# Transform along H with one load of y for both parts, two column halves in two PSUM banks, and the inverse along H beside the first MLP product

## The chip, the cores and the metric

The kernel runs on one core of a Trainium2 chip. The metric is the device time of one execution in microseconds (us). TensorE (PE) multiplies out of SBUF into PSUM, which has eight banks; VectorE (DVE) and ScalarE (ACT) empty PSUM; GpSimd (POOL) works on SBUF; SyncE (SP) issues nearly all DMAs. Everything is float32, and the profile shows every float32 matmul as two records, and as many weight loads (PEld).

## The reference

Two layers work on an image x of 2 x 768 x 64 x 64 (batch, channel, height H, width W). Layer 0 is a convolution block with a state space scan; the change does not touch it. Layer 1 is a spectral MLP:

```python
xf = rfft2(groupnorm(x), norm='ortho')            # 64 x 33 frequencies, complex
xr, xi = xf.real, xf.imag                         # 32 blocks of 24 channels
x1r = relu(xr @ w1[0] - xi @ w1[1] + b1[0])       # 24 -> 96 in each block
x1i = relu(xi @ w1[1] + xr @ w1[0] + b1[1])
x2r = softshrink(x1r @ w2[0] - x1i @ w2[1] + b2[0])
x2i = softshrink(x1i @ w2[1] + x1r @ w2[0] + b2[1])
x = x + irfft2(complex(x2r, x2i), norm='ortho')
```

Each Fourier transform is a product with a constant 64-point matrix: along W, then along H, and back in the other order.

## The kernel before, in words

`layer0` fills some three quarters of the time. `layer1` begins at about 3405 us. All its instructions are written in the order in which each engine runs them (`tc.manual_schedule()`), so an engine works strictly down its list, and waits where an operand or a buffer is not ready.

**Ahead of the loop** (3405 to 3515 us) the list `forward_w(0)` takes image 0 through the transform along W: 16 slabs of four rows, each loaded by SP (L585), normalized on DVE in six instructions (L624, tile fx), transposed on PE (pt, L635), copied to SBUF (xc), multiplied by the matrix fw (py, L642), copied to yw and stored to DRAM (yspec, L645). pt and py use PSUM tiles of the tag "aux" with three buffers. `evict` (L610, L612) copies them out, in turn on DVE and on ACT.

**The loop** has 192 steps. A *group* is six columns of W frequencies (`KWS`) of one image; the last group of an image has three, and the first one of an image begins with the frequencies 0 and 32, whose spectrum along W is real (`g.real`), so their columns of y hold 64 rows and not 128. A group has 16 steps (hp), each with two of the 32 channel blocks. Step n does, in this order:

1. `hidden` of step n: the first MLP product, ph (L798), four matmuls from zf, in 64-row halves of the array, into three banks; then bias and relu into hid, on ACT (L807, two) and DVE (L805, one).
2. `spectrum` of step n+1: the transform along H. For each column j, y's 64 channels are the stationary operand, and the real and imaginary halves of the matrix fh are the moving one, 64 elements each. The two matmuls of a column write the two partition halves of one PSUM tile, mz (tag "pz", one bank, L769). Four copies bring it into zf: two on DVE (L783), two on ACT (L785), written in the order DVE, ACT, ACT, DVE.
3. `out` of step n-1: the second MLP product, mo (L814), three matmuls for each of up to three pieces. Between the pieces stand the `bits`, a share of a background list: during the first 72 steps `forward_w(1)` (pt and py of image 1, as above), from step 112 on `inverse_w(0)` (ipo, L683, added to the image by DVE, L687, and stored). Steps 72 to 111 and the last have none.
4. `shrink` of step n-1: bias on DVE (L831), soft shrink on POOL (L836, L837) into z.

Once a group is done, `inverse_h` goes through the next group's even steps from hp 2 on: each call multiplies two columns of z, in the two row halves of the array, by the inverse matrix ih (pv, L729: four matmuls of 384 moving elements into two aux tiles), and `evict` copies them into vo, one on DVE and one on ACT; every second call stores vo on SP (L744, L746). The call stands in the middle of that step's bits, and thus between pieces of mo, or behind the last piece where there are no bits.

The last group's `inverse_h` and `inverse_w(1)` follow the loop as a tail (from about 4597 us).

PSUM before: aux 3 banks, mz 1, ph 3, mo 1, eight in all.

Of the kernel before, what the change touches and what calls it, by code (L numbers as in the profile page):

```python
# [9 lines left out]
F32 = mybir.dt.float32  # L10
# [5 lines left out]
B, DM, H, W = 2, 768, 64, 64  # L16
# [10 lines left out]
NHP, KG, DP = 16, 6, 32 * 32  # L27
# [4 lines left out]
def spectral_kernel(tc, a, out):  # L32
# [5 lines left out]
    with ExitStack() as top:  # L38
# [56 lines left out]
        with ExitStack() as ctx:  # L95
            layer1(ctx, tc, a, x1_d, y_d, v_d, outr, ident, gm1, gr1)
# [465 lines left out]
def layer1(ctx, tc, a, x1_d, y_d, v_d, outr, ident, gm1, gr1):  # L562

    nc = tc.nc
# [4 lines left out]
    ps = ctx.enter_context(tc.tile_pool(name="ps1", bufs=1, space=PSUM))  # L569
    fw = wp.tile([128, 128], F32, name="fw")  # L570
    fh = wp.tile([128, 128], F32, name="fh")
# [11 lines left out]
    def load_slab(b, q):  # L583
        slabs[b, q] = p2.tile([128, NCT, 256], F32, tag="slab", name=f"fx_{b}_{q}", bufs=5)
        nc.sync.dma_start(slabs[b, q], x1_d[b][:, :, q * 256 : (q + 1) * 256])  # L585
# [26 lines left out]
            nc.scalar.copy(out, psum)  # L612

    def aux(shape, name):
        return ps.tile(shape, F32, tag="aux", name=name, bufs=3)


    def forward_w(b):
# [9 lines left out]
        def turn_over(k, g):  # L628
            if g == 0:
                cols[k] = p2.tile([128, DM], F32, tag="xc", name=f"xc_{b}_{k}")  # L630
            xt = slabs[b, k // 2]
            pt = aux([128, 3, 128], f"pt_{b}_{k}_{g}")
            for j in range(3):
                at = (k % 2) * 128
                nc.tensor.transpose(pt[:, j, :], xt[:, 3 * g + j, at : at + 128], ident)  # L635
            evict(cols[k][:, g * 384 : (g + 1) * 384], pt.rearrange("p j c -> p (j c)"))

        def transform(k, g):
            rows[k] = yws[k % 3]
            py = aux([128, 384], f"py_{b}_{k}_{g}")  # L640
            half = slice(g * 384, (g + 1) * 384)
            nc.tensor.matmul(py, fw, cols[k][:, half], start=True, stop=True)  # L642
            evict(rows[k][:, 16 * g : 16 * g + 16, :GC], py.rearrange("p (n c) -> p n c", c=GC))
            if g == 1:
                nc.sync.dma_start(  # L645
                    y_d[b][2 * k : 2 * k + 2].rearrange("h k c -> (h k) c"),
                    rows[k].rearrange("p n c -> p (n c)"),
                )
# [19 lines left out]
    def inverse_w(b):  # L668
        last = L // 256
        vs, xs = {}, {}  # L670

        def load(q):
            vs[q] = p2.tile([128, 2, DM], F32, tag="slab", name=f"iv_{b}_{q}", bufs=5)
            xs[q] = p2.tile([128, NCT, 256], F32, tag="slab", name=f"ix_{b}_{q}", bufs=5)
            nc.sync.dma_start(  # L675
                vs[q], v_d[b][4 * q : 4 * q + 4].rearrange("(k h) w c -> (h w) k c", h=2)
            )
            nc.sync.dma_start(xs[q], x1_d[b][:, :, q * 256 : (q + 1) * 256])  # L678

        def transform(q, ct):  # L680
            po = aux([128, 2, 128], f"ipo_{b}_{q}_{ct}")
            for k in range(2):
                nc.tensor.matmul(  # L683
                    po[:, k, :], vs[q][:, k, ct * 128 : (ct + 1) * 128], iw, start=True, stop=True
                )
            xt = xs[q][:, ct, :]
            nc.vector.tensor_add(xt, xt, po.rearrange("p k t -> p (k t)"))  # L687
            if ct == NCT - 1:
                nc.sync.dma_start(outr[b, :, :, q * 256 : (q + 1) * 256], xs[q])  # L689

        todo = [lambda: load(0)]
        for q in range(last):
            if q + 1 < last:
                todo.append(lambda q=q: load(q + 1))
            for ct in range(NCT):
                todo.append(lambda q=q, ct=ct: transform(q, ct))
        return todo
# [58 lines left out]
    class Step:  # L756
# [4 lines left out]

        def spectrum(self):
            g, nk = self.g, len(self.g.kws)
            pz = ps.tile([128, KG, H], F32, tag="pz", name=f"mz_{self.n}")
            for j in range(nk):
                kn = H if g.real[j] else 128
                cols = g.y[:kn, j, self.hp * 64 : self.hp * 64 + 64]
                for ri in range(2):
                    nc.tensor.matmul(  # L769
                        pz[64 * ri : 64 * ri + 64, j, :],  # L770
                        cols,
                        fh[:kn, ri * H : (ri + 1) * H],
                        start=True,
                        stop=True,
                    )
            self.zf = p3.tile([128, KG * H], F32, tag="zf", name=f"zf_{self.n}")
            for ri in range(2):
                for e in range(2):
                    to = slice(64 * e + 32 * ri, 64 * e + 32 * ri + 32)
                    src = pz[64 * ri + 32 * e : 64 * ri + 32 * e + 32, :nk, :]  # L780
                    dst = self.zf[to, : self.nt]
                    if e == ri:
                        nc.vector.tensor_copy(dst, src.rearrange("p j h -> p (j h)"))  # L783
                    else:
                        nc.scalar.copy(dst, src.rearrange("p j h -> p (j h)"))  # L785

        def hidden(self):
            nt = self.nt
# [54 lines left out]
    def at(n):  # L843
        return steps[n] if 0 <= n < len(steps) else None

    with tc.manual_schedule():
        for do in forward_w(0):
            do()
        load_slab(1, 0)
        groups[0].load()  # L850
        later = {0: forward_w(1), per + NHP: inverse_w(0)}
        pace = {0: 5 * NHP - 8, per + NHP: 4 * NHP + 2}
        fill, todo, given, begun = [], [], 0, 0
        groups[1].load()
        steps[0].spectrum()
        for n in range(len(steps) + 2):
            now, before, after = at(n), at(n - 1), at(n + 1)
            gi, hp = divmod(n, NHP)
            if n in later:
                assert given == len(todo)  # L860
                todo, given, begun, span = later[n], 0, n, pace[n]
            due = min(len(todo), -(-len(todo) * (n + 1 - begun) // span))
            bits = todo[given:due]
            given = due
            if hp == 2 and gi > 0:
                fill = groups[gi - 1].inverse_h()
            if hp >= 2 and hp % 2 == 0 and fill:
                bits.insert(len(bits) // 2, fill.pop(0))
            if hp == 1 and 0 < gi and gi + 1 < len(groups):
                groups[gi + 1].load()  # L870
            if now is not None:
                if hp == 0:
                    now.g.open()
                now.hidden()
            if after is not None:
                after.spectrum()
            cuts = [len(bits) * i // 4 for i in range(5)]
            for j in range(4):
                for do in bits[cuts[j] : cuts[j + 1]]:
                    do()  # L880
                if before is not None and j < 3 and 128 * j < before.nt:
                    before.out(j)
            if before is not None:
                before.shrink()
        for do in groups[-1].inverse_h():
            do()
        assert given == len(todo)
        for do in inverse_w(1):
            do()
# [96 lines left out]
```

## Time and profile before

| | us |
|---|---|
| median of three runs | 4713.02 (4712.79 to 4720.27) |
| profiled execution | 4721.7, span 4719.9 |
| PE busy | 4416.7 (94%) |
| weight loads (PEld) busy | 3224.1 (68%) |
| DVE busy | 3714.8 (79%) |
| ACT busy | 2349.2 (50%) |
| POOL busy | 922.3 (20%) |
| mz, L769: records, mean | 3968 of form 128\*64 at 227 ns, 256 of form 64\*64 at 238 ns |
| zf copies of 32x384 | DVE 320 at 554 ns, ACT 320 at 470 ns |
| zf copies of 32x192 | DVE 64 at 355 ns, ACT 64 at 310 ns |
| pv, L729 | 528 records of 64 rows, mean 508 ns |

A form like 128\*64 names the rows and columns of the array that a matmul uses. Records of one group overlap: two matmuls in different parts of the array run at the same time, and a record's duration includes the time until its last result is out. The time that a run of matmuls takes is therefore read from the start of its first record to the start of the next run's first. The share of busy time is an average over stages with different limits, and the two layers have little in common.

### The profile page before, as it was taken

How to read it: one execution, taken by the hardware profiler on the slowest of the kernel's cores; microseconds unless marked ns; L12 is line 12 of the kernel's file. 1: busy time of each engine (PE TensorE's matmuls, PEld its weight loads, DVE VectorE, ACT ScalarE, POOL GpSimd, SP SyncE). 2: the span in 40 equal slices, each digit the busy share in tenths (PEclk: the TensorE clock that was granted, in tenths of full speed). 3: DMA queues.
4: the chain of work that ended last, by engine and by line, in shares of the span. 5: the costliest groups of instructions: out<-in, count | busy, mean ns of one | idle time of the engine just before them, and what ended most of it. 6: DMA issues, size and time to landing. Idle time of an engine off the chain costs nothing. (4 is left out here: it accounts for less than half of the span.)

```text
span 4719.9 us, 78500 instructions
## 1 busy us (share of the span) xinstructions
PE 4416.7 (94%) x28368; PEld 3224.1 (68%) x28368; DVE 3714.8 (79%) x5630; ACT 2349.2 (50%) x4811; POOL 922.3 (20%) x1681
## 2 busy tenths in 40 slices
PE   5989999999999999999999999996679999999995
PEld 4567666777777677777777777774547666777774
DVE  4499999899999999899999999998455555444443
ACT  0365555565656656566566665664024444433330
POOL 1022211122222211122222222221201112222220
PEclk9999999999999999999999999998789999999998
DMA  6567777566666666566666666662383442346429
GB/s 235 172 184 216 219 216 211 180 199 200 207 196 194 201 192 207 168 202 204 204 207 192 204 203 202 195 188 84 138 272 103 114 127 82 81 130 175 134 75 330
DMA packets 517665, 854.31 MB, mean 181 GB/s; under 512 B 60369, under 2 KB 402017, under 8 KB 510113
## 3 DMA queue, kind: packets, MB, share of 16 engines
q1 hardware_dynamic: 514208, 833.66, 58.8%
q0 software_dynamic: 3072, 15.63, 0.9%
q8 instruction: 229, 3.75, 0.3%
q14 instruction: 156, 1.27, 0.1%
HBM read 606.87 MB, written 114.03 MB: 153 GB/s over the span
## 5 line engine op out<-in xcount | busy, mean ns | idle before, releaser
L444 PE MATMUL po<-y,wo 128*128 128x256 f32 x4608 | 1084.2, 386 | 92.1 <-DVE o L455 92.1
L245 PE MATMUL pi<-x,wi 128*128 128x256 f32 (+2 forms) x4608 | 1090.0, 386 | 1.1 <-ACT x L226 1.1
L444 PEld LDWEIGHTS po<-y,wo 128*128 128x128 f32 x4608 | 886.3, 193 | 251.2 <-DVE o L455 113.9
L245 PEld LDWEIGHTS pi<-x,wi 128*128 128x128 f32 x4608 | 851.5, 191 | 217.6 <-issue 102.2
L373 DVE TENSOR_TENSOR_SCAN hs<-da,hs 128x1028 f32<-128x1028 f32 x384 | 883.3, 2300 | 46.6 <-DVE hs L369 0.5
L352 ACT ACTIVATE da<-dl,acol 128x256 f32<-128x256 f32 x1536 | 639.9, 497 | 2.6 <-DVE hs L373 1.1
L284 PE MATMUL pc<-pair,wc 128*64 128x256 f32 x4608 | 594.0, 390 | 21.1 <-DMA pair<-win 10.9
L383 POOL TENSOR_TENSOR hc<-hc 128x512 f32<-128x512 f32 x384 | 488.4, 1272 | 605.1 <-DVE hc L382 595.6
L377 POOL COPY state<-hs 128x4 f32<-128x4 f32 x360 | 104.6, 291 | 1985.2 <-DVE hs L373 1985.2
L783 DVE COPY zf<-mz 32x384 f32<-32x384 f32 (+1 forms) x384 | 200.0, 521 | 368.0 <-ACT zf L785 185.2
L284 PEld LDWEIGHTS pc<-pair,wc 128*64 128x64 f32 x4608 | 305.5, 137 | 268.9 <-issue 149.8
L382 DVE TENSOR_TENSOR hc<-hs,bc 128x1024 f32<-128x1024 f32 x384 | 468.0, 1219 | 0.0
L369 DVE TENSOR_TENSOR hs<-du,bc 128x1024 f32<-128x1024 f32 x384 | 465.7, 1213 | 0.7 <-DMA bc<-bc_d 0.7
L260 ACT COPY win<-pi 128x256 f32<-128x256 f32 (+2 forms) x384 | 137.9, 359 | 654.9 <-PE pi L245 613.8
L297 DVE SCALAR_TENSOR_TENSOR pc<-win,vec,pc 128x256 f32<-128x256 f32 x768 | 373.7, 487 | 83.9 <-PE pc L284 66.9
L814 PE MATMUL mo<-w,hid 128*128 128x96 f32 (+1 forms) x3264 | 435.8, 279 | 0.7 <-DVE v L831 0.7
L814 PEld LDWEIGHTS mo<-w,hid 128*128 128x128 f32 (+1 forms) x3264 | 391.2, 189 | 52.2 <-issue 25.6
L807 ACT ACTIVATE hid<-ph,b 128x384 f32<-128x384 f32 (+1 forms) x384 | 212.7, 555 | 307.6 <-PE ph L798 306.6
L798 PE MATMUL ph<-zf,w 64*128 64x384 f32 (+3 forms) x1536 | 316.4, 496 | 3.6 <-ACT zf L785 3.6
L345 ACT ACTIVATE dl<-pz,vec 128x256 f32<-128x256 f32 x384 | 170.5, 473 | 214.8 <-PE pz L341 212.1
L836 POOL TENSOR_SCALAR cl<-v 128x288 f32<-128x288 f32 (+1 forms) x224 | 85.0, 380 | 933.3 <-DVE v L831 920.9
L785 ACT COPY zf<-mz 32x384 f32<-32x384 f32 (+1 forms) x384 | 170.3, 443 | 170.9 <-DVE zf L783 168.6
(119 smaller groups left out, 4909.8 us busy)
## 6 DMA issues: line engine op xcount, KB each, us to landing
wi<-in_win_dram SPq DMA_DIRECT2D x384, 384.0 KB
wo<-wout_d SPq DMA_DIRECT2D x192, 768.0 KB
pair<-win SPq DMA_DIRECT2D x1536, 66.0 KB
wc<-in_wcv_dram SPq DMA_DIRECT2D x384, 192.0 KB
bc<-bc_d SPq DMA_DIRECT2D x32, 1024.0 KB
yspec<-yw SPq DMA_DIRECT2D x64, 512.0 KB
xo<-in_x_dram SPq DMA_DIRECT2D x192, 128.0 KB
x<-o SPq DMA_DIRECT2D x192, 128.0 KB
```

What stands on the lines that cost most here:

```text
L245: nc.tensor.matmul(self.pi[:, : self.tn], self.win[dt][:, ct, :], self.x[:, ct, : self.tn], start=(ct == 0), stop=(ct == NCT - 1),)
L284: nc.tensor.matmul(pc[64 * h : 64 * h + 64, :T], self.wcv[dt][:, h, dx, :], pair[:, h, :, dx : dx + W], start=(dx == 0), stop=(dx == 2),)
L297: nc.vector.scalar_tensor_tensor(acc if dx < 2 else u, wins[dt][:, 2 : 2 + ROWS, dx : dx + W], vec[:, dt, 6 + dx : 7 + dx], acc, ALU.mult, ...
L352: nc.scalar.activation(das[dt % 4][:, s, 1:], self.dl[dt], AF.Exp, scale=acol[:, dt, s : s + 1])
L369: nc.vector.tensor_mul(hs[:, :, 1:], self.du.unsqueeze(1).to_broadcast([128, NS, T]), self.bc[:, :NS, :])
L373: nc.vector.tensor_tensor_scan(flat, self.da[dt].rearrange("p s t -> p (s t)"), flat, 0.0, ALU.mult, ALU.add)
L382: nc.vector.tensor_mul(hc, hs, self.bc[:, NS:, :])
L383: nc.gpsimd.tensor_add(hc[:, 0:2, :], hc[:, 0:2, :], hc[:, 2:4, :])
L444: nc.tensor.matmul(self.po[ct][:, :T], self.out[ct][0][:, dt, :], self.y[dt], start=(dt == 0), stop=(dt == NDT - 1),)
L798: nc.tensor.matmul(to, w1[rows, self.hp, cols], self.zf[rows, :nt], start=True, stop=True)
L807: nc.scalar.activation(hid, ph[q][:, :nt], AF.Relu, bias=bias)
L814: nc.tensor.matmul(self.po[:n, j, :], self.hid[:, q, j * 128 : j * 128 + n], w2[:, self.hp, q, :], start=(q == 0), stop=(q == 2),)
```

## The change

`aux` gets two buffers, and mz two tiles (tags pz0 and pz1), so PSUM stays at eight banks.

`spectrum` does one matmul for each column, with the whole of fh (128 elements) as the moving operand, so both parts come from one load of y. The columns are split in two halves of hk (three of six, two and one of three). The first half writes partitions 0 to 63 of pz0, the second half partitions 64 to 127 of pz1, and they are issued in turns: j = 0, 3, 1, 4, 2, 5, or 0, 2, 1. A tile holds real and imaginary parts side by side, so each copy into zf takes 32 partitions with three runs of 64: four copies of pz0 on DVE, four of pz1 on ACT.

In the loop, a call of `inverse_h` is taken out of the bits, and stands between `hidden` and `spectrum`.

```diff
     def aux(shape, name):
-        return ps.tile(shape, F32, tag="aux", name=name, bufs=3)
+        return ps.tile(shape, F32, tag="aux", name=name, bufs=2)
...
-            pz = ps.tile([128, KG, H], F32, tag="pz", name=f"mz_{self.n}")
-            for j in range(nk):
-                kn = H if g.real[j] else 128
-                cols = g.y[:kn, j, self.hp * 64 : self.hp * 64 + 64]
-                for ri in range(2):
-                    nc.tensor.matmul(
-                        pz[64 * ri : 64 * ri + 64, j, :],
-                        cols,
-                        fh[:kn, ri * H : (ri + 1) * H],
-                        start=True,
-                        stop=True,
-                    )
+            pz = [
+                ps.tile([128, KG // 2, 2, H], F32, tag=f"pz{i}", name=f"mz_{self.n}_{i}")
+                for i in range(2)
+            ]
+            hk = (nk + 1) // 2
+            for j in sorted(range(nk), key=lambda j: j % hk):
+                kn, side = H if g.real[j] else 128, 64 * (j // hk)
+                nc.tensor.matmul(
+                    pz[j // hk][side : side + 64, j % hk].rearrange("p r h -> p (r h)"),
+                    g.y[:kn, j, self.hp * 64 : self.hp * 64 + 64],
+                    fh[:kn, :],
+                    start=True,
+                    stop=True,
+                )
             self.zf = p3.tile([128, KG * H], F32, tag="zf", name=f"zf_{self.n}")
-            for ri in range(2):
+            for side, ks in ((0, hk), (1, nk - hk)):
                 for e in range(2):
-                    to = slice(64 * e + 32 * ri, 64 * e + 32 * ri + 32)
-                    src = pz[64 * ri + 32 * e : 64 * ri + 32 * e + 32, :nk, :]
-                    dst = self.zf[to, : self.nt]
-                    if e == ri:
-                        nc.vector.tensor_copy(dst, src.rearrange("p j h -> p (j h)"))
-                    else:
-                        nc.scalar.copy(dst, src.rearrange("p j h -> p (j h)"))
+                    for ri in range(2):
+                        to = slice(64 * e + 32 * ri, 64 * e + 32 * ri + 32)
+                        rows = slice(64 * side + 32 * e, 64 * side + 32 * e + 32)
+                        src = pz[side][rows, :ks, ri, :]
+                        dst = self.zf[to, side * hk * H : (side * hk + ks) * H]
+                        dst = dst.rearrange("p (j h) -> p j h", h=H)
+                        if side == 0:
+                            nc.vector.tensor_copy(dst, src)
+                        else:
+                            nc.scalar.copy(dst, src)
...
-            if hp >= 2 and hp % 2 == 0 and fill:
-                bits.insert(len(bits) // 2, fill.pop(0))
...
                 now.hidden()
+            if hp >= 2 and hp % 2 == 0 and fill:
+                fill.pop(0)()
             if after is not None:
                 after.spectrum()
```

## The prediction

> **What bounds the kernel now.** I read the busy time by stage first, since the page's averages mix two layers. The changed code runs in the last quarter of the span (4719.9 us; the profiled execution took 4721.7 us, 8.7 us above the median of 4713.02, so I add differences to the median).
>
> ```profile
> 3405.00:3515.00 110.00, 90.20 (x320) 49.37 (x320) 69.36 (x160) 30.68 (x64) 6.05 (x2) 0.90 0.73 259
> 3552.00:4590.00 1038.00, 1036.68 (x10028) 736.18 (x10028) 517.75 (x1092) 433.55 (x876) 230.05 (x430) 1.00 0.41 114
> ```
>
> Columns: stretch, length, busy time of PE, weight loads, DVE, ACT, POOL, then granted clock, DMA share, GB/s. In the second row, the loop over 192 steps, PE works 1036.68 of 1038 us at full clock and the others half the time: a step costs what its matmuls cost, gaps between shapes included. The first row is the transform along W ahead of the loop: no engine full, so there a handover counts.
>
> Then PE in order of time (start, duration, line, x records; each f32 matmul is two records). A plain step with its inverse, then two short-filled steps, then a step of the group with the real frequencies 0 and 32:
>
> ```profile
> 4208.11 1.56 PE L729 MATMUL pv<-z,ih 64*128 64x384 f32 x8
> 4209.60 0.91 PE L814 MATMUL mo<-w,hid 128*128 128x96 f32 x6
> 4210.44 1.71 PE L798 MATMUL ph<-zf,w 64*128 64x384 f32 x8
> 4212.08 0.92 PE L769 MATMUL mz<-fh,y 128*64 128x64 f32 x24
> 4212.93 2.25 PE L814 MATMUL mo<-w,hid 128*128 128x96 f32 x18
> ```
> ```profile
> 3980.60 1.56 PE L729 MATMUL pv<-z,ih 64*128 64x384 f32 x8
> 3982.00 1.60 PE L798 MATMUL ph<-zf,w 64*128 64x384 f32 x8
> 3983.53 0.92 PE L769 MATMUL mz<-fh,y 128*64 128x64 f32 x24
> 3984.38 2.25 PE L814 MATMUL mo<-w,hid 128*128 128x96 f32 x18
> 3986.56 1.82 PE L798 MATMUL ph<-zf,w 64*128 64x384 f32 x8
> 3988.31 0.92 PE L769 MATMUL mz<-fh,y 128*64 128x64 f32 x24
> ```
> ```profile
> 4128.78 0.49 PE L798 MATMUL ph<-zf,w 64*64 64x384 f32 x2
> 4129.10 1.01 PE L769 MATMUL mz<-fh,y 64*64 64x64 f32 x22
> 4130.04 1.13 PE L814 MATMUL mo<-w,hid 128*128 128x96 f32 x8
> ```
>
> Start to start, mz takes 0.85 us (4212.08 to 4212.93). With three columns (12 records, 4043.91 to 4044.41) it takes 0.50. So a matmul with 64 moving elements costs 0.35/6 = 0.058, one column half beside the other, and a change of array shape (rows*columns ahead of the operand sizes) costs a fixed 0.15: the drain, and a weight load with nothing beside it. The inverse pv shows the same price: a step with pv between two mo lasts 6.80 (4191.29 to 4198.09) where its like without lasts 5.14 (4210.44 to 4215.58), 1.66 for a pv of 1.49, so the extra change costs 0.16-0.17.
>
> **The change, term by term.**
>
> *a. Six matmuls of 128 moving elements for twelve of 64.* The moved elements stay the same. The weight loads that halve lie under the streaming. Price of one pass with 128 columns beside another: the inverse along W (128x128 moving) adds 0.45 us to a step for 4 records (5.59 against 5.14), 0.112 each; layer 0's convolution, also two 64-column halves side by side, has passes of 256 every 0.216, which with the 0.058 interpolates to 0.111. mz becomes 6 x 0.111 + 0.15 = 0.815, 0.035 less. 128 plain steps: -4.5 us. Bounds: 0.70 per mz (no cost but 6 x 0.107 by length, and half the fixed part) and 0.92 (the convolution group's mean of 0.129 per record), -19 to +9; the interpolated row is nearest.
>
> One rule here reads otherwise. The Trainium skill, "TensorEngine Tiling (Array Packing)", Instruction Overhead, states about 60 cycles per matmul on TRN2. Taken as lost time on each record (25 ns at the 2.4 GHz of "TensorE: Matmul & The Clock Gate"), six fewer pairs would save an estimated 0.15 us per step, 19 us in this term, and the sum below would be +9 instead of +24. The measured 0.058 and 0.216 leave only about 5 ns per pass that does not scale with length, so I go by them.
>
> *b. Real groups: 64-row and 128-row matmuls now alternate.* Columns 0 and 1 of groups 0 and 6 contract 64 rows (the 64*64 form), the other four 128. Today j runs 0,0,1,1,2..5: one change inside mz, and from 4129.10 to mo 0.94 us. The new order is 0,3,1,4,2,5, so rows go 64,128,64,128,128,128: three changes, and columns 0, 3 and 1 run alone, since two shapes do not share the array. From the same point: j0, j3, j1 alone, then j4 beside j2, then j5 = 5 x 2 x 0.111 = 1.11, plus 3 x 0.15 of changes, plus the 0.10 drain ahead of mo = 1.66. That is +0.72 per step. The first of 32 steps waits for DMA anyway: 31 x 0.72 = +22.5 us. Bounds: if shapes overlapped freely, 3 pairs x 0.222 + 0.15 = 0.82, -4 us; if each change cost 0.25, +32.
>
> *c. Groups of three columns:* halves of 2 and 1, so 4 passes of 0.111 + 0.15 = 0.59 against 0.50: 32 x 0.095 = +3 us.
>
> *d. pv moved between ph and mz.* 64 calls fall in the loop. 45 of them now stand between two mo: there pv costs 1.65, and in its new place 1.49 (ph ends in another shape, mz starts in another anyway): 45 x -0.16 = -7.2. The other 19 stand at the end of a step with nothing else to fill it; the next ph has pv's shape and takes 1.53 (3982.00 to 3983.53) instead of 1.64. These pay 1.28 now and 1.49 after: +4.0; four of them in group 6 also part ph from the 64*64 mz that overlaps its end today: +0.6. The stores of vo go out some 2 us earlier on SP, ahead of that step's slab loads; what they write is read many steps later. z's last POOL write is over a step old by then. pv's two evictions sit on DVE and ACT ahead of the zf copies, but mz (0.82) covers their 0.56 and 0.48.
>
> *e. zf copies.* Today they form one chain, DVE 0.55, ACT 2 x 0.47, DVE 0.56 over one bank, ending 2.24 after mz; a bare mo (2.18) just fails to cover it, which is the 1.75 for 1.64 at 3986.56. 39 steps wait some 0.12: 5 us. After, two banks: DVE four copies of 32x192, ACT four. This form takes 355 and 310 ns in the three-column groups, so 0.12 + 1.42 = 1.54 us, under every mo: -5. DVE gains 0.31 and ACT 0.30 us per step, both at half load. If the split rows (3 x 64) cost like the full 384, 4 x 0.55 + 0.12 = 2.32: the wait stays, +1.
>
> *f. Two aux buffers for three, before the loop.*
>
> ```profile
> 3499.56 2.03 DVE L624 TENSOR_SCALAR fx<-fx,gm,gr 128x256 f32<-128x256 f32 x6 [0.18 <-DMA fx<-x]
> 3501.50 0.56 DVE L610 COPY xc<-pt 128x384 f32<-128x384 f32 x1
> 3502.66 0.56 DVE L610 COPY yw<-py 128x384 f32<-128x384 f32 x1 [0.60 <-PE py L642]
> 3503.68 0.56 DVE L610 COPY xc<-pt 128x384 f32<-128x384 f32 x1 [0.47 <-PE pt L635]
> 3504.78 0.56 DVE L610 COPY yw<-py 128x384 f32<-128x384 f32 x1 [0.54 <-PE py L642]
> ```
>
> A slab now takes 5.7 to 6.1 us, or about 7.2 where the clock dips, 6.45 on average (14 slabs, 3415.20 to 3505.49). With two buffers DVE always empties one and ACT the other, and DVE's becomes a serial chain: normalization to end of xc 2.50, then py 0.95 + copy 0.56, pt 0.63 + 0.56, py 0.95 + 0.56, four handovers of 0.05: 6.9 us. 16 slabs x 0.46 = +7.5, say +8. Bounds: 0 (loads decide anyway, the wait of 0.18) and +28 (half clock throughout, 8.3 per slab). The clock was 0.50 at full PE load from 3488.6 to 3491.9, after a PE wait of 2.16 us; the new waits are 0.5 to 0.8.
>
> On that, "TensorE: Matmul & The Clock Gate", Part 1, wants an idle window of about 3.4 us before the clock drops, more than the 2.16 that this trace shows. By its rule the new gaps never cost clock, by the row they have a margin of 1.2 us: both leave +8.
>
> *In the loop* a buffer comes round after two other items, at least 1.6 us, for 0.2 + 0.56 of eviction, or 2.2 us behind the zf copies in the worst slot; hidden. With that cover gone, 0.1 on each of some 350 tiles would be +35.
>
> *g. Tail.* The last group's pv calls need both buffers (4597.39 on): the third column's second half waits for the first's copy, +1.2 us ahead of the inverse. The inverse along W there alternates with DMA at about 0.9 of its share; a slab's last sums come 0.5 later in some 8 links of the chain, partly hidden: +1.5 (0 to 4).
>
> Sum: -4.5 + 22.5 + 3 - 7.2 + 4.6 - 5 + 8 + 2.7 = +24 us, 0.5%; 4713 + 24 = 4737.
>
> **Rivals.** (1) The alternation costs nothing: other row groups overlap after all. For it: at 4123.66 an mz record already starts under ph's last pair. Against: that pair has mz's shape, 64*64, and mo waits out a drain after every mz. Price: b is -4 instead of +22.5, sum -2: 4711, not slower. It decides once b is under 8 us, 0.26 per step. (2) The first stage falls to half clock: f is +28, sum +44: 4757. For it: the clock already dips three times there. Against: the longest gaps get shorter, since the loads come earlier against the slower slabs. (3) The zf copies or the two buffers stall the loop: +0.1 on the tiles that share the evictions of the steps, about 150 of them, and e lost: +20 more, 4757. Against: DVE and ACT are idle half the loop.
>
> **How the numbers follow.** Chances: forecast 0.64, rival 1 0.16, rival 2 0.11, rival 3 0.09. The measurement can tell about 0.2%, 9.4 us, from no change. The forecast's own range is 4722 to 4750 (terms a and f at half their bounds); about 0.04 of it ends below +9.4. Rival 1 splits, 0.08 within and 0.08 faster, as term a may add a few microseconds. So faster 0.08, same 0.13, slower 0.79. The range 4715 to 4759 takes in rivals 2 and 3 and the upper half of rival 1.
>
> **What would show it.** mz in real groups near 1.6 us from ph's end to mo with the forms 64*64 and 128*64 alternating; plain mz 0.82; pv 1.49 between ph and mz; no ph waiting for zf; DVE and ACT copying zf at the same time for 1.4 us; slabs of 6.9 us before the loop. Wrong if real mz stays under 1.2 us, if PE is idle at pt, py or pv in the loop, or if the first stage is under half clock.

## The result, and the profile after

The changed kernel takes 4741.38 us (median of 6 runs, 4735.09 to 4744.13) against 4720.0 for the kernel before (6 runs, 4712.79 to 4723.94): 1.0048 times as long, 95% interval 1.0038 to 1.0059. That is +21 us, where the prediction's sum was +24. The profiled execution has a span of 4742.4 us against 4719.9, +22.5.

I cut each span in four: the *stage* from the first normalization of this layer to the first hid row (the transform along W ahead of the loop, the group's load, the first transform along H); the *start*, the loop's first four steps; the *rest of the loop*, from step 4 to the last step's first hid row on ACT; and the *tail*. The times are read from the starts of the normalization's and hid's records (the rows of tile hid in experiment 8 give the first start, and as last start that of the last step's second hid row, 0.4 to 0.6 us behind the point that I use).

| us | stage | start | rest of the loop | tail |
|---|---|---|---|---|
| before | 127.9 | 27.4 | 1031.7 | 126.7 |
| after | 135.2 | 31.4 | 1035.1 | 136.0 |
| difference | +7.3 | +4.0 | +3.4 | +9.3 |

So over two thirds of the loss lie outside the loop, whose matmuls the change rewrites. The loop's +7.4 are two large terms of opposite sign: its two groups with real frequencies got 19.3 us longer, the two three-column groups 4.0 longer, and the other eight groups 15.9 us shorter.

The stretches of the kernel after, in the columns of the stretches shown for before (the busy time of PE, weight loads, DVE, ACT and POOL, then granted clock, DMA share, GB/s), the stage's and the loop's:

```profile
3405.00:3515.00 110.00, 94.84 (x310) 44.29 (x311) 66.75 (x157) 29.18 (x61) 4.42 (x2) 0.95 0.68 240
3552.00:4590.00 1038.00, 1038.00 (x7908) 706.91 (x7910) 575.80 (x1447) 484.55 (x1235) 227.22 (x420) 1.00 0.41 114
```

PE's records in the loop fall from 10028 to 7908, and its busy time does not: the stretch is as full as before. In the stage the granted clock went up (0.95 from 0.90), so the stage is not longer because of its clock.

A step of the first real group of the second batch, PE in order of time, kernel after (start, duration, line, x records): without the inverse, and with it.

```profile
4125.35 1.71 PE L803 MATMUL ph<-zf,w 64*128 64x384 f32 x8
4126.89 1.68 PE L771 MATMUL mz<-fh,y 64*64 64x128 f32 x12
4128.50 2.25 PE L819 MATMUL mo<-w,hid 128*128 128x96 f32 x18
4130.68 1.71 PE L803 MATMUL ph<-zf,w 64*128 64x384 f32 x8
4132.32 1.55 PE L729 MATMUL pv<-z,ih 64*128 64x384 f32 x4
4133.81 1.73 PE L771 MATMUL mz<-fh,y 64*64 64x128 f32 x12
4135.47 2.25 PE L819 MATMUL mo<-w,hid 128*128 128x96 f32 x18
```

From mz to mo it is 1.61 us (4126.89 to 4128.50), where the step of before in the prediction took 0.94 from the same point (4129.10 to 4130.04): +0.67 a step. In mz's single records columns 0, 3 and 1 start one after another (4126.89, 4127.20, 4127.56), and only columns 4 and 2 start together (4127.92). From ph to mo it is 3.15; run 7 below, with the old order and the new copies, takes 2.48, and most such steps of before took 2.59, as ph waited 0.11 for zf. Where pv stands ahead it takes 1.49 (4132.32 to 4133.81), as it was costed.

The stage's slabs after, on DVE (an idle time in brackets ends with its releaser):

```profile
3496.71 2.02 DVE L624 TENSOR_SCALAR fx<-fx,gm,gr 128x256 f32<-128x256 f32 x6
3498.64 0.55 DVE L610 COPY xc<-pt 128x384 f32<-128x384 f32 x1
3500.20 0.56 DVE L610 COPY yw<-py 128x384 f32<-128x384 f32 x1 [1.00 <-PE py L642]
3501.45 0.56 DVE L610 COPY xc<-pt 128x384 f32<-128x384 f32 x1 [0.70 <-PE pt L635]
3503.02 0.56 DVE L610 COPY yw<-py 128x384 f32<-128x384 f32 x1 [1.01 <-PE py L642]
3503.49 2.02 DVE L624 TENSOR_SCALAR fx<-fx,gm,gr 128x256 f32<-128x256 f32 x6
```

This slab takes 6.78 us from normalization to normalization (3496.71 to 3503.49); over 14 slabs the mean is 6.86, before 6.45. It is the serial chain of the prediction: DVE now waits 1.00 us for each py, where before it waited 0.54 to 0.60, and this slab's normalization doesn't wait for its load any more.

The zf copies of after by tile (duration min/median/max in ns, first and last start):

```profile
L788 DVE COPY zf<-mz x768: 278/347/356, 3535.2 to 4605.2; 32x192 f32<-32x192 f32 x160, 32x128 f32<-32x128 f32 x32
L790 ACT COPY zf<-mz x768: 204/311/313, 3537.5 to 4604.9; 32x192 f32<-32x192 f32 x160, 32x64 f32<-32x64 f32 x32
```

Four of 0.347 and four of 0.311 run at the same time, 1.4 us in place of the chain of 2.24.

### The profile page after: what moved, and what is told of

It reads as the page before. It is cut to its first block, busy times and chain, and to the rows that moved or that the text cites. A ratio compares the mean times of both kernels' runs of the same rounds, so it can differ in the third digit from the quotient of the medians.

```text
span 4742.4 us, 75218 instructions
## 1 busy us (share of the span) xinstructions
PE 4445.9 (94%) x26256; PEld 3204.0 (68%) x26256; DVE 3779.6 (80%) x6014; ACT 2404.4 (51%) x5195; POOL 921.6 (19%) x1681
## 5 line engine op out<-in xcount | busy, mean ns | idle before, releaser
L284 PE MATMUL pc<-pair,wc 128*64 128x256 f32 x4608 | 593.7, 389 | 19.3 <-DMA pair<-win 5.7
L788 DVE COPY zf<-mz 32x192 f32<-32x192 f32 (+1 forms) x768 | 259.9, 338 | 169.8 <-PE mz L771 158.5
L790 ACT COPY zf<-mz 32x192 f32<-32x192 f32 (+1 forms) x768 | 225.3, 293 | 97.1 <-PE mz L771 87.7
```

The costliest lines, as they stand in the source:

```text
L284: nc.tensor.matmul(pc[64 * h : 64 * h + 64, :T], self.wcv[dt][:, h, dx, :], pair[:, h, :, dx : dx + W], start=(dx == 0), stop=(dx == 2),)
L788: nc.vector.tensor_copy(dst, src)
```

## The experiments

The theory after the result: the loss is the alternation of 64-row and 128-row matmuls (+22) and the second auxiliary buffer outside the loop (+7 and +9); the two-bank copies give back more than was counted. The runs below are told in the order of the question. "Before" is run beside each on the same chip.

**1. The real groups' order alone, in the kernel after (pair_real).**

```diff
-            for j in sorted(range(nk), key=lambda j: j % hk):
-                kn, side = H if g.real[j] else 128, 64 * (j // hk)
+            for j in range(nk):
+                kn, side = H if g.real[j] else 128, 64 * (j % 2)
...
-                    pz[j // hk][side : side + 64, j % hk]...
+                    pz[j % 2][side : side + 64, j // 2]...
```

The zf copies put the columns back in place by a strided destination.

> The changed kernel, but column j goes to tile j mod 2 and the columns are issued as 0, 1, 2, 3, 4, 5: the two 64-row columns run side by side, and the array's row count changes once inside mz instead of three times. Theory (the alternation of 64 and 128 rows is the main cost): in the two real groups ph and mz together take about 2.5 us per step instead of 3.15 (1.54 + 1.61), 31 x 0.65 = 20 us less than the changed kernel, so about 4720, a ratio of 1.000 to the kernel before. Plain and three-column steps stay at 4.62 and 3.06. Rival (the loss is mostly in the stages outside the loop, where two buffers serve instead of three): under 8 us gained, 4733 or more.

4720.76 us, 1.0008 times before (0.9998 to 1.0017). Groups 0 and 6 went from 104.64 and 90.44 us to 92.57 and 80.11, together -22.4; group 5 got 0.7 shorter too, as its last step already runs the first transform of group 6, and the other groups and the tail kept their times within 0.4 us. That is 23.1 us of loop, of which the start, the first four steps, has 4.2; from step 4 on it is 18.9 for 27 real steps, 0.70 each. A step of group 6 now, on PE:

```profile
4098.34 0.49 PE L803 MATMUL ph<-zf,w 64*64 64x384 f32 x2
4098.66 0.96 PE L771 MATMUL mz<-fh,y 64*64 64x128 f32 x10
4099.56 2.25 PE L819 MATMUL mo<-w,hid 128*128 128x96 f32 x18
```

Five columns in 0.90 us (one mz matmul already ran beside ph's last pair). The order of the columns is the whole of term b, and with it mended the change is level with before. By the times it is worth some 19 us (1.0048 to 1.0008).

**2. The same order in the kernel before (alt_before):** `for j in (0, 3, 1, 4, 2, 5)` for six columns. Here every column still has its real and its imaginary half side by side, so only the two further changes of shape are added, and no column runs alone.

> The kernel before, with nothing changed but the order of the columns in the transform along H: 0, 3, 1, 4, 2, 5 instead of 0 to 5, both halves of a column still side by side. It has two more changes of row count in a real step, and no column that runs alone. Theory (a change costs a drain and an exposed weight load, 0.15 us, and the rest of the real groups' 0.67 us is columns that run alone): +0.30 us per real step, 31 steps, +9 us, ratio 1.002. Rival 1 (a change costs 0.33 and nothing else counts): +20 us, 1.0044. Rival 2 (changes are free, only running alone costs): 0, 1.000.

4728.05 us, 1.0020 (1.0011 to 1.0030). Group 6 went from 81.48 to 85.89 us: 4.41 in 16 steps, 0.28 a step, 0.14 for each extra change of shape. So of the 0.67 that a real step lost, 0.28 is the changes and the remaining 0.39 the columns that have no neighbour of their shape.

**3. Two auxiliary buffers alone, in the kernel before (aux2_before):** `bufs=3` to `bufs=2`.

> The kernel before with two aux buffers instead of three, one PSUM bank left unused. Theory (the two buffers cost what the trace of the changed kernel shows outside the loop): slabs ahead of the loop of 6.8 us, +7 us; tail +9 us; loop unchanged within 1 us; sum +16, ratio 1.0035. Rival (the tail got longer from the half clock that follows later and longer waits, or from how the runs fall, not from the buffers): tail as before, +7 us in all, 1.0015. Second rival (the loop suffers too, matmuls waiting for a buffer): over +20.

4767.53 us, 1.0107 (1.0091 to 1.0124): far over the +16 that stage and tail explain, so it is the second rival that came true. These two, 135.5 (+7.6) and 136.2 (+9.5), were as after; but the rest of the loop took 1061.9 us, 30 more. The loop pays as well, and the place shows in a step of this run (PE in order of time):

```profile
4196.26 0.64 PE L683 MATMUL ipo<-iw,iv 128*128 128x128 f32 x4
4196.74 0.81 PE L814 MATMUL mo<-w,hid 128*128 128x96 f32 x6
4197.47 2.35 PE L729 MATMUL pv<-z,ih 64*128 64x384 f32 x8
4199.75 0.91 PE L814 MATMUL mo<-w,hid 128*128 128x96 f32 x6
```

pv takes 2.28 us (4197.47 to 4199.75) in place of 1.49: it fills two buffers at once, and the piece right ahead of it, here ipo, still holds one. Over the loop, from pv's starts to the next matmul's, that adds 26.7 us to before, most of the 30. The kernel after doesn't show this, although it has two buffers. What differs is where pv stands.

**4. The move of pv alone, in the kernel before with three buffers (pv_before):**

```diff
-            if hp >= 2 and hp % 2 == 0 and fill:
-                bits.insert(len(bits) // 2, fill.pop(0))
...
                 now.hidden()
+            if hp >= 2 and hp % 2 == 0 and fill:
+                fill.pop(0)()
```

> The kernel before with only the inverse along H moved to between ph and mz. Theory: 45 calls save 0.16 us each (-7.2), 19 at a step's end lose 0.21 (+4.0), and those steps then wait for zf's one-bank chain, 0.12 each (+2): about -1 us, ratio 0.9998. Rival (the call in the middle of mo gave cover to evictions or to zf, which is lost): +5 or more, with PE waiting in ph.

4720.86 us, 1.0007 (0.9997 to 1.0016). Groups 1 to 3 and 7 to 10, where pv stood between two mo, gain 5.1 us; groups 5, 6 and 11, where it stood at the step's end, lose 5.4; group 4 has calls of both kinds and loses 0.5. From step 4 on the loop has 1032.5 us against 1031.7: +0.8. With three buffers the move is worth nothing.

**5. The move with two buffers, in the kernel before (pv_aux2_before):** both edits, 3 and 4.

> The kernel before with two auxiliary buffers and with pv moved next to the first MLP product; transform, zf copies and column order as before. Without the move two buffers cost the loop 28 us (and 17 outside it, 4767.5 us); the changed kernel's loop with pv put back lost only 8 us. Theory: pv's place alone is what makes two buffers bearable: the loop within 4 us of the run that moved pv alone with three buffers (1062 us from the first hid to the last), stage and tail longer by 8 and 9 us: 4735 to 4742 us, 1.003 to 1.005. Rival: the old zf copies, 0.55 us long, hold the evictions up as well, and the two-bank copies are the other half of it: the loop 10 to 20 us longer than 1062, 4748 to 4758 us.

4738.9 us, 1.0046 (1.0032 to 1.0060). The rest of the loop is 1033.4 us, 0.9 more than with three buffers (1032.5), where run 3 had 1061.9. So with pv at its new place giving up the third buffer is all but free in the loop; stage 136.5 and tail 137.0 carry its price. The rival, that the new zf copies are the other half of it, is out for pv at its new place.

**6. The counter-check in the changed kernel (mid_pv):** run 1 with pv put back in the middle of the pieces.

> The run with the columns parted over the sides (4720.8 us), with pv put back in the middle of the step's auxiliary pieces, where the kernel before has it; two buffers as in the changed kernel. Theory: moving pv is worth nothing with three buffers (4720.9 against 4717.7 us) but is what lets the loop live with two: pv fills both at once and has to wait until the copies of the pieces right ahead of it are done. In the kernel before with two buffers this cost the loop some 28 us, so here +20 to +30 us, 4741 to 4751 us, and pv's records at 2.2 us and more in place of 1.49. Rival: those 28 us came from the transform's own pieces colliding with the old zf copies, and the new copies (half on each engine, 0.35 and 0.31 us) leave room: then +0 to +5 us, 4721 to 4726 us.

4735.83 us, 1.0032 (1.0020 to 1.0044): +15 on run 1, or +11 by the two ratios, as before was 4 us longer beside it too; that lies between the two expectations. The rest of the loop took 1027.8 against 1016.2 us, +11.7, and PE's records show the same wait, here one of the longest, 2.19 us from pv to mo:

```profile
3683.45 0.91 PE L642 MATMUL py<-xc,fw 128*128 128x384 f32 x2
3684.20 0.80 PE L819 MATMUL mo<-w,hid 128*128 128x96 f32 x6
3684.93 2.26 PE L729 MATMUL pv<-z,ih 64*128 64x384 f32 x8
3687.12 0.91 PE L819 MATMUL mo<-w,hid 128*128 128x96 f32 x6
```

The mechanism holds; its size here is 12 us and not the 28 between runs 3 and 5, and for the pieces of the inverse along W the trace shows the zf copies to be why. Where pv stands behind ipo, the sum over ipo is what frees the buffer. In run 3 that sum queues on DVE behind the last zf copy of the one-bank chain and ends 1.95 us after ipo began; in run 6 the copies are done sooner, and it ends 1.25 us after. pv then waits 0.79 us in run 3 and 0.09 in run 6. Over the loop the waits add 8.4 us to before's time of pv (run 3: 26.7). Outside, run 6's stage and tail are 3.1 and 3.7 us longer than run 1's, and its start is 3.7 us shorter; I have no cause for these.

**7. Two matmuls of 64 columns again, copies out of two banks as after (two_banks):** run 1 with the real parts into one bank and column half, the imaginary parts into the other. Each engine now makes two zf copies of 384 columns in place of four of 192.

```diff
-                nc.tensor.matmul(
-                    pz[j % 2][side : side + 64, j // 2]...,
-                    g.y[...], fh[:kn, :], ...)
+                for ri in range(2):
+                    nc.tensor.matmul(
+                        pz[ri][64 * ri : 64 * ri + 64, j, :],
+                        g.y[...], fh[:kn, ri * H : (ri + 1) * H], ...)
```

> The run with the columns parted over the sides (4720.8 us), but with two matmuls of 64 moving columns for each tile of y, as in the kernel before, the real part into the one bank and column half, the imaginary part into the other; the two-bank copies stay, VectorE taking the real parts and ScalarE the imaginary parts whole. So it undoes the part 'both parts through one loaded tile' alone. Theory: 12 short matmuls take 0.85 us in a step of a group without real columns where 6 long ones take 0.81: 128 such steps x 0.04 = +5 us; in the three-column groups 6 short ones on two halves take 0.50 against 0.58, 32 x -0.08 = -2.6; real groups within 2 us; together +1 to +5 us, 4722 to 4726 us. Rival: what made the plain groups 2.6 us shorter was the single load of y and not the copies; then undoing it gives back most of the plain groups' -16 us: 4733 to 4738 us.

4728.26 us, 1.0015 (1.0005 to 1.0024); the interval overlaps that of run 1. That is 2 us over the range expected, and the profiled execution (4720.63) is the shortest of ten. The steps tell more than the time: mz 0.85 us in place of 0.81 in a plain step, 0.50 in place of 0.58 in a three-column step, both as expected, and every plain group 0.55 to 0.7 us longer. From step 4 on the loop has 1019.7 us against 1016.2: +3.5, the worth of the single load of y; mz's own times account for it.

This run differs from run 5 in the loop by the two-bank copies (and the order of the columns' halves is that of before), so the two measure term e: 1033.4 to 1019.7, **-13.7 us** from step 4 on. The end of step 41, the zf copies and what they delay, in run 5, with one bank:

```profile
3794.39 0.55 DVE L783 COPY zf<-mz 32x384 f32<-32x384 f32 x1 [0.22 <-PE mz L769]
3794.97 0.95 ACT L785 COPY zf<-mz 32x384 f32<-32x384 f32 x2 [0.84 <-DVE zf L783]
3795.96 0.56 DVE L783 COPY zf<-mz 32x384 f32<-32x384 f32 x1 [1.02 <-ACT zf L785]
3796.53 0.74 DVE L624 TENSOR_SCALAR fx<-fx,gm,gr 128x256 f32<-128x256 f32 x2
3796.66 1.00 PE L635 MATMUL pt<-ident,fx 128*128 128x128 f32 x3
3797.59 1.71 PE L798 MATMUL ph<-zf,w 64*128 64x384 f32 x8
```

The same of this run, with two banks:

```profile
3781.26 1.11 DVE L786 COPY zf<-mz 32x384 f32<-32x384 f32 x2 [0.98 <-PE mz L772]
3781.30 0.97 ACT L788 COPY zf<-mz 32x384 f32<-32x384 f32 x2 [0.29 <-PE mz L772]
3782.38 0.73 DVE L624 TENSOR_SCALAR fx<-fx,gm,gr 128x256 f32<-128x256 f32 x2
3783.54 0.49 PE L635 MATMUL pt<-ident,fx 128*128 128x128 f32 x3
3783.96 1.39 PE L801 MATMUL ph<-zf,w 64*128 64x384 f32 x6
```

With one bank, DVE idles 1.02 us for ACT's part of zf, starts its last copy at 3795.96, and the next slab's normalization queues behind it; PE's transposes (pt) then take 0.93 us (3796.66 to 3797.59) where 0.42 is their work. With two banks DVE is through at 3782.37, and the normalization is done before pt's turn. Compared step by step from step 4 on, nine steps of run 5 end with such a late pt (4.5 us together), and in 65 steps ph takes about 0.12 longer, the wait for zf (7.9 us). Before has six such late pt (3.0 us) and 40 such waits (5.4 us): the move of pv alone, run 4, brings both to the numbers of run 5, as more steps then end in a bare mo.

**8. Spare banks outside the loop (spare_banks):** run 1, and ahead of the loop and behind it, where ph0 to ph2 lie idle, the auxiliary products use their banks too.

```diff
     def aux(shape, name):
-        return ps.tile(shape, F32, tag="aux", name=name, bufs=2)
+        tags = ("aux", "aux", "ph0", "ph1", "ph2") if outside[0] else ("aux",)
+        tag = tags[count[0] % len(tags)]
+        count[0] += 1
+        return ps.tile(shape, F32, tag=tag, name=name, bufs=2 if tag == "aux" else 1)
```

> This is the earlier run with the real and the complex columns parted over the two sides (4720.8 us, so level with the kernel before), with one more edit: ahead of the loop and behind it, where the banks of ph0, ph1 and ph2 lie idle, the auxiliary products go round five buffers (the two of aux, then those three) where they had two. Theory: the first stage lost 7 us (last row of the layer-0 transform's first step at 3539.9 against 3534.2 with a like start) and the tail 9.3 us (136.0 against 126.7) to the second buffer alone, because a product can no longer be written while the copy of the one before and the sum over it still run. Then both come back whole, and with five more than the three of before a little more than whole: the first stage -7 to -9, the tail -9 to -11, the loop as it was; 4702 to 4705 us, 0.997 of the kernel before. Rival: the tail is longer because its rows of the spectrum come later (the loads, not the buffers), and the first stage because of the order of the prefetched work; then the time stays at 4719 to 4721.

4703.4 us, 0.9963 (0.9950 to 0.9976). Stage 124.7 (-10.3), tail 125.1 (-10.6), the rest of the loop 1016.2 as it was. Both losses were the second buffer's. The rows of tile hid on ACT (duration in ns, first and last start), kernel after:

```profile
L812 ACT ACTIVATE hid<-ph,b x384: 420/580/585, 3539.9 to 4606.8; 128x384 f32<-128x384 f32 x160, 128x192 f32<-128x192 f32 x32
```

and this run, whose lines are numbered five higher from there on:

```profile
L817 ACT ACTIVATE hid<-ph,b x384: 420/580/583, 3528.8 to 4570.5; 128x384 f32<-128x384 f32 x160, 128x192 f32<-128x192 f32 x32
```

The tail's chain of what ended last, one slab of before (start, duration, what):

```profile
4618.35 0.43 DVE ix L687
...
4618.82 1.62 PE ipo L683 x12
...
4620.46 0.43 DVE ix L687
```

A slab of after, and the load behind it:

```profile
4648.29 0.43 DVE ix L687
...
4648.77 0.73 PE ipo L683 x4
...
4649.52 0.43 DVE ix L687
...
4650.00 1.17 PE ipo L683 x8
...
4651.19 0.43 DVE ix L687
...
4652.07 8.83 DMA iv<-vspec
```

The same chain with five buffers:

```profile
4649.19 1.26 DVE ix L692 x4
...
4650.52 0.76 DVE ix L692 x2
...
4652.61 9.31 DMA ix<-x
```

After, a slab's products and sums take turns (add 0.43, product 0.73, add, product 1.17, add), because a product can't be written while the sum over its buffer runs; and the next load is issued only when the last sum is done. With five buffers the products of this slab are finished ahead, and the chain here has sums and loads alone.

**9. Spare banks for the kernel before (spare_before),** six buffers outside the loop, nothing else.

> The kernel before, whole, with one edit: ahead of the loop and behind it the auxiliary products go round six buffers (the three of aux, then the idle banks of ph0, ph1 and ph2). It tells how much of the gain of the run with five buffers (0.9963) belongs to spare banks as such and how much to the change without its two costs. Theory: three buffers were all but enough (a stage of 128.0 us from the first norm to the first hid, a tail of 126.7 us, against 124.7 and 125.1 with five), so the spare banks give before 3 us in the stage and 2 us in the tail: 4712 to 4718 us, 0.998 to 0.9995; the change itself, with its columns parted and with spare banks, is then worth some 12 to 15 us. Rival: before gains as much as the changed kernel did (20 us), 4700 us, and the change in the loop is worth nothing.

4718.02 us, 0.9999 (0.9990 to 1.0008): level. In its profile the stage is 0.7 us shorter, the rest of the loop equal and the tail 3.0 shorter. Three buffers were all but enough, so run 8's gain isn't the spare banks as such: it is the rest of the change, once its two costs are taken out.

**10. pv last in the steps without pieces (late_pv),** run 8 with

```diff
-                fill.pop(0)()
+                if bits:
+                    fill.pop(0)()
+                else:
+                    bits.append(fill.pop(0))
```

> As the run with five buffers outside the loop, but the inverse along H (pv) goes beside the first MLP product only in the steps that carry auxiliary pieces; in the steps that carry none of them it goes last in the step, as in the kernel before, since in the trailing steps pv beside ph cost 1.8 us a group (59.43 against 57.67 and 83.36 against 81.48 in the run that moved pv alone). Theory: the steps that pv is moved back in gain about 0.2 us each, 19 of them, so -4 us: about 4700 us, 0.996 of the kernel before. Rival: with two buffers in the loop, pv behind other pieces waits for both of them to be copied (2.2 to 2.9 us in place of 1.49 in the run of before with two buffers), and each such step loses 0.7 to 1.4 us in place of gaining 0.2: 10 to 25 us longer than the run with five buffers.

4705.28 us, 0.9961 (0.9948 to 0.9974): not to be told from run 8 by time. In its profile groups 4, 5, 6 and 11 are 4.4 us shorter, as expected, and the rest of the loop 1011.7; but in that profile the layer began 7.3 us later than in run 8's, and the stage was 4.8 us longer at a clock of 0.84 in its first 110 us against 0.92. The time doesn't show the gain, the steps do.

**11. All of it (best):** run 10, and in the two three-column groups alone the two matmuls of run 7.

> The run with five buffers outside the loop and pv beside the first product only in steps that carry auxiliary pieces (4705.3 us in one run, its loop 4.4 us shorter than with pv always beside ph), and in the two three-column groups alone the transform by two matmuls a column, real part in the one bank and half, imaginary part in the other, as in the run that undid this part (0.50 in place of 0.58 us in a step). Theory: 32 steps x 0.08 = -2.4 us: groups of 56.7 and 54.6 us where they were 57.9 and 55.9; the loop from the first hid to the last 1036 us; the time 4695 to 4703 us, 0.995 to 0.9965 of the kernel before. Rival: the loop is shorter as told, but the start of the layer (its stage began up to 7 us later in one profile than in another of the same code) moves as much as the gain: 4703 to 4708 us, not to be told from the run with five buffers.

4694.23 us (5 runs, 4691.38 to 4698.06), 0.9951 (0.9939 to 0.9964), the fastest here and better than both kernels: the rest of the loop 1009.1 us, groups 5 and 11 at 56.65 and 54.61.

## Why the prediction was right

The time was right: +24 forecast, +21 measured, the sign and the likeliest case too. Of its terms four stand and three were off. That the three errors (+3.4, -8.7 and +6.6) nearly cancel is luck.

| term | predicted, us | measured, us | by |
|---|---|---|---|
| a, c: one load of y, three columns | -1.5 | -3.5 | runs 7 and 1, from step 4 on |
| b: real groups' order | +22.5 | +23.1 | run 1, 4.2 of it in the start |
| d: pv moved | -2.6 | +0.8 | run 4, from step 4 on |
| e: two-bank zf copies | -5 | -13.7 | runs 5 and 7, from step 4 on |
| f: two buffers, stage | +8 | +7.3 | before, after; run 8 gives it back |
| f: two buffers, loop | 0 | +0.9 | runs 4 and 5 |
| g: two buffers, tail | +2.7 | +9.3 | before, after; run 8 gives it back |

Their sum is 24.2; stage, loop and tail together grew by 24.0 in the profiles (the span by 22.5, since this layer began 1.6 us earlier). The agreement is no test of the rows: the loop's follow one chain of runs (before, 4, 5, 7, 1, after), so they add up of themselves. Rows a, c, d and e and the loop's row of f leave out the first four steps, which vary from 21.6 to 31.4 us over all these runs; the start's share is in row b, as these steps are real ones.

Three of the prediction's sums are a little off, and nothing hangs on them: 31 x 0.72 is 22.3, not 22.5; 6 x 0.107 and half of 0.15 make 0.72, not 0.70, as term a's lower bound; and 16 slabs of 8.3 us would cost +30, not +28.

- **Terms a and c.** mz 0.81 for 0.815 predicted in a plain step, 0.58 for 0.59 with three columns. Interpolating the duration of a 128-column pass from neighbouring rows worked. The rule of the Trainium skill ("TensorEngine Tiling (Array Packing)", Instruction Overhead), taken as lost time, would have made a plain step an estimated 0.15 us shorter; it got 0.04 shorter.
- **Term b.** mz to mo +0.67 a step for +0.72 predicted, and run 2 parts it as the prediction did: the changes of shape at 0.14 each (0.15 predicted), the rest columns alone. The row's +23.1 is nearer to +22.5 than the steps earn: from step 4 on it is 18.9, where 27 steps of 0.72 would be 19.4, and the start's 4.2 belong to the stretch that varies most. Rival 1 (the alternation costs nothing) is out.
- **Term d.** The price was right and the waits behind it were left out. In groups 7 to 10 the 24 moved calls gained 0.17 us each, for 0.16 predicted. But run 4 also has 25 more waits of ph for zf and three more late pt than before, 3.7 us together; without them +0.8 would be -2.9. The two-bank copies take these waits away again, so the 3.7 stand against row d and for row e. The larger miss is one of structure: the term stood by itself, at three buffers. With two, the move is worth 28 us (runs 3 and 5), since it takes pv away from pieces that hold a buffer. "In the loop a buffer comes round after two other items ... hidden" was true only because of the move, and the prediction didn't say so.
- **Term e.** The step that failed is "39 steps wait some 0.12: 5 us". It counted ph's waits in before, rightly; but with pv moved, more steps end in a bare mo: 65 waits, 7.9 us (run 5 against run 7). And it missed that normalizations queue on DVE behind the last zf copy: 4.5 us of late transposes, 3.0 of them already in before. The two make 12.4 of the 13.7. The two-bank copies are the best part of the change.
- **Term f, stage.** 6.78 us a slab (6.86 in the mean) for 6.9 predicted, +7.3 for +8, and the clock held, at 0.95. Rival 2 (half clock) is out.
- **Term g.** The 1.2 us ahead of the inverse came in size: from the last step's first hid row to the first load of iv 15.2 us for 14.0. (pv itself took 1.6 longer, in two waits and not one, and the stretch behind it 0.4 less.) The step that failed is "a slab's last sums come 0.5 later in some 8 links, partly hidden: +1.5 (0 to 4)": from that load to the end it was +8.2. A link got 0.79 us longer (0.43 + 0.73 + 0.43 + 1.17 + 0.43 against 0.43 + 1.62 + 0.43, with the handovers 3.33 against 2.54), and nothing hid it, since the next load waits for the slab's last sum. The granted clock was lower too. The stretch from the last start of hid to the end (length, busy time of PE, weight loads, DVE, ACT, POOL, granted clock, DMA share, GB/s), kernel before:

```profile
4593.80:4719.90 126.10, 71.28 (x432) 62.03 (x432) 40.25 (x103) 1.86 (x4) 3.22 (x11) 0.83 0.90 309
```

Kernel after:

```profile
4606.80:4742.40 135.60, 84.12 (x432) 73.39 (x432) 41.54 (x104) 1.85 (x4) 3.30 (x11) 0.74 0.86 288
```

Run 8, with five buffers:

```profile
4570.50:4695.10 124.60, 74.34 (x432) 67.43 (x432) 38.55 (x103) 1.84 (x4) 3.27 (x11) 0.79 0.91 313
```

The same 432 matmul records took 84 us of PE at a granted clock of 0.74, where before took 71 at 0.83. Five links of the chain after have the longer form, some 4 us. How much of the rest is turns and how much clock, these runs don't part; with five buffers the clock is 0.79, under that of before, and the tail is the shorter for all that, with DMA at a share of 0.91.

Rival 3 (the zf copies or the two buffers stall the loop) is out for this change, but only just: stalls on the buffers are what happens when pv stays where it was (run 3).

## What to carry to other kernels

Keep matmuls with different row counts apart in the order of issue and give each column half the same mix, for every change of shape cost about 0.14 us here, and a matmul without a neighbour of its shape cost the pair's time alone. A buffer given up for one stage has to be priced in every stage that shares the pool, by the chain product, copy, next product; where other banks lie idle in that stage, they can stand in. A copy that two engines made from one bank was a chain here: count who queues behind its last link, not only who waits for its output.

## What the runs showed of the hardware

The copies of one PSUM bank by DVE and ACT never ran side by side in the kernel before: of its 384 zf copies on each engine no two overlap (DVE 0.55 us, then ACT 0.95, then DVE 0.56 in the lines of run 5). Of two banks they did (1.11 and 0.97 us, begun 0.04 us apart, in the lines of run 7). The profile names the other engine's copy as what each waited for, as far as it infers that from semaphores; whether the chip itself would ask for this order, these runs don't tell. In the tail the same 432 matmul records, spread over 9.5 us more, ran at a granted clock of 0.74 in place of 0.83.
